# Products over 64 rows, issued once per batch and group of heads instead of once per pair of tiles, in a post-norm transformer block

## The chip, the cores and the metric

The kernel runs on one core of a Trainium2 chip. The core has a matrix engine (TensorE, "PE" in the profile, whose weight loads are a row of their own, "PEld"), three engines for element-wise work (VectorE "DVE", ScalarE "ACT", GpSimd "POOL") and a queue for transfers (SyncE "SP"). Each engine executes its own instructions in the order in which they were emitted, and waits on semaphores for the others. The metric is the device time of one execution in microseconds (us). Three runs of the kernel before gave 1061.97, 1062.08 and 1062.28 us; the median is 1062.08 us.

## The reference

One transformer layer in float32 on an input of 2 batches, 512 tokens and 512 features:

```
q, k, v = x @ Wq.T, x @ Wk.T, x @ Wv.T     # 32 query heads, 8 key/value heads, 128 wide
q, k = rmsnorm(q) * q_norm_w, rmsnorm(k) * k_norm_w
scores = q k / sqrt(128) + slope[head] * (key_pos - query_pos), later keys masked
out = softmax(scores) @ v                  # four query heads share a key/value head
x = layernorm(x + out @ Wo.T)
h = silu(x @ gate.T * gate_s) * (x @ up.T * up_s)       # 1376 wide, integer weights
x = layernorm(x + h @ down.T * down_s)
```

## The kernel before

**Tiling.** The 1024 tokens are 8 tiles of 128 rows, four per batch. A *unit* is (g, b, i): key/value head g (0 to 7), batch b, query tile i (0 to 3) of that batch. Two neighbouring units form a *pair*; there are 64 units and 32 pairs, so a batch and a group g have two pairs: tiles 0 and 1, then tiles 2 and 3. For each pair the main loop (from L1271) emits the projection to q, k and v (`project`), the norms and transposes (`heads`), then for each unit the scores with their softmax (`scores`) and the weighted sum of the values (`attend`), and then the output projection of the pair (`project_out`), which adds into the residual `y`. With the last head, g = 7, the pair's two tiles are normalised (`norm1`). Groups 0 to 5 are visited with the batches inside the group; the last two groups are visited batch by batch. The feed-forward part follows, and its first blocks for batch 0 are placed beside the end of the attention of batch 1.

**Seven products for eight.** Projections (`project`, `project_out`, the feed-forward parts) use Strassen's scheme in Winograd's form (`seven`, L616): seven products of half-sized blocks in place of eight, with sums of operands made on DVE or POOL ahead (for `project_out` the sums `so`, made from `aT` by `sums_a`) and products added up as they leave the accumulators. Product after product goes to one of three accumulator banks a, b, c (`pa_o`, `pb_o`, `pc_o` for the output projection), and each product is added into `y` by DVE (L576) before its bank takes the next one that starts afresh.

**Attention over 64 rows.** A unit's own diagonal block of scores is lower triangular in four strips of 32 queries. For the strips of queries 0 to 63 only the first 64 keys count, for the strips of queries 64 to 127 all 128 keys do. So the product of the diagonal block with the values is split: `attend` multiplies with all 128 rows only for the later queries (L1063), and for the earlier queries of *both* units of a pair the 64 key rows are packed into the two halves of the partitions: `scores` writes the even unit's block into rows 64 to 127 of the odd unit's buffer (`pr_of[i + 1]`, keys `"x"`), they are transposed together into one `prT` tile, and at the end of the odd unit `halves` (L1093) issues two products with 64 rows each, at `tile_position=(k * H2, 0)`: rows 0 to 63 hold the odd unit's block and give its part of the output in bank `px`, rows 64 to 127, against values that were copied to these rows of `vs`, give the even unit's part in bank `pz`; each product is 256 columns wide. `px` is then added into `aT` by DVE, and `pz` is copied (first tile of a batch) or added. The two products of a pair write two different banks: `px` from the ring of transposes `pt` (two banks) and `pz` from the ring `po` (one bank), which also holds `pa`, the accumulator of `attend`.

**What sets the order.** `W.add` records each operation with a planned cost per engine, a priority and the buffers that it reads and writes. `Work.emit` then simulates the engines with these planned costs and emits the operations in the order that results, choosing the engine where an operation may go to more than one (`copy_op`, `tensor`). A buffer is taken from a ring (`ring(stage, name, bufs, shape)`) when its first operation is emitted, and only if a slot is free. So sizes of rings, costs and priorities shape the order on every engine. The program that results is fixed; on the chip, nothing is planned.

**Rings touched.** `kT` and `v` hold keys and values of one (g, b); `prT` (5 slots) the transposed probabilities; `aT` the attention output of a pair; `vs` the shifted values of a pair.

Of the kernel before, what the change touches and what calls it, by code (L numbers as in the profile page):

```python
# [13 lines left out]
ALU = mybir.AluOpType  # L14
# [3 lines left out]
P = 128  # L18
B, S, DM = 2, 512, 512
H, HKV, HD = 32, 8, 128  # L20
G = H // HKV
# [3 lines left out]
NTB = S // P  # L25
# [5 lines left out]
NQ = P // Q  # L31
# [3 lines left out]
H2 = P // 2  # L35
# [12 lines left out]
def pe(n):  # L48
    return max(0.14, n / 600)
# [5 lines left out]
def act(n, scaled=False):  # L55
    return 0.15 + 0.00084 * n + (0.1 if scaled else 0.0)


def dve(n):
    return 0.15 + 0.00106 * n  # L60


def pool_tt(n):
    return 0.27 + 0.00197 * n
# [197 lines left out]
def post_ln_block(  # L262
# [18 lines left out]
    nc = tc.nc  # L281
# [4 lines left out]
    W = Work()  # L286
# [13 lines left out]
    def ring(stage, name, bufs, shape, dtype=F32, gate=None):  # L300
        r = Ring(name, bufs, shape, dtype, gate)
        rings.setdefault(stage, []).append(r)
        return r
# [33 lines left out]

    r_wo = ring("att", "wo", 2, [P, G, DM])
    r_to = ring("att", "to", 1, [P, 4, 2, WO])
    r_kT = ring("att", "kT", 3, [P, S])  # L340
    r_v = ring("att", "v", 3, [P, NTB, HD])
    r_qT = ring("att", "qT", 6, [P, NQ, G, Q])
    r_bias = ring("att", "bias", 2, [P, S])
    r_prT = ring("att", "prT", 5, [P, S])
    r_aT = ring("att", "aT", 2, [P, 2, G, P])
    r_so = ring("att", "so", 1, [P, 4, 2, P])
    r_rel = ring("att", "rel", 1, [P, S])
    r_vs = ring("att", "vs", 2, [P, HD])
    r_pr = [ring("att", f"pr{i}", 1, [P, NQ, (i + 1) * P]) for i in range(NTB)]

    for stage, side in (("all", "left"), ("qkv", "left"), ("att", "right")):
# [12 lines left out]
    A = lambda buf: (buf, 0)  # L364
# [5 lines left out]
    pairs = units[::2]  # L370
# [90 lines left out]
    def load_o(g, prio):  # L461
        wo = Buf(r_wo, f"wo_{g}")
        w_o[g] = wo
        load(
            1.05,
            prio,
            lambda q: q.dma_start(wo.tile, wot[ts(g, G * HD), :].rearrange("(h p) c -> p h c", p=P)),
            [A(wo)],
        )
# [60 lines left out]
    for i in range(NTB):  # L530
# [3 lines left out]
            lambda e, i=i: nc.vector.memset(pr_of[i].tile, 0.0),  # L534
# [36 lines left out]
    def tensor(n, prio, dst, a, b, alu, reads, writes, who=("DVE", "POOL"), sbuf=None, after=()):  # L571
        cost = {"DVE": dve(n), "POOL": pool_tt(n)}
        W.add(
            {e: cost[e] for e in who},
            prio,
            lambda e: vec[e].tensor_tensor(dst(), a(), b(), alu),  # L576
            reads,
            writes,
            after,
            port=len(who) > 1 if sbuf is None else sbuf,  # L580
        )
# [115 lines left out]
    c_of, qTs, kTs, vs, v2s, prTs, aTs = {}, {}, {}, {}, {}, {}, {}  # L697

    def copy_op(n, prio, dst, src, reads, writes, who=("ACT", "DVE")):
        def fn(e):  # L700
            if e == "ACT":
                nc.scalar.copy(dst(), src())  # L702
            else:
                vec[e].tensor_copy(dst(), src())  # L704

        cost = {"ACT": act(n), "DVE": dve(n), "POOL": 0.18 + 0.00086 * n}
        W.add({e: cost[e] for e in who}, prio, fn, reads, writes)
# [316 lines left out]
    def attend(u, prio):  # L1024

        g, b, i = u  # L1030
        key = f"{g}_{b}_{i}"
        pr, v = pr_of[i], vs[g, b]
        p, r = divmod(units.index(u), 2)
        for j in range(i + 1):
            pt, prT = Buf(r_pt, f"pt_{key}_{j}"), Buf(r_prT, f"prT_{key}_{j}")
            prTs[u, j] = prT
            tiles = (2, 3) if j == i and r == 0 else (2, 3, 0, 1) if j == i else (0, 1, 2, 3)
            reads = [(pr, a) for a in tiles]
            if j == i and r:
                reads += [(pr, ("x", a)) for a in range(2)]  # L1040

            def transposes(e, j=j, pt=pt, tiles=tiles):
                for k, a in enumerate(tiles):
                    nc.tensor.transpose(pt[:, ts(k, P)], pr[:, a, ts(j, P)], ident.tile)  # L1044

            n = len(tiles)
            W.add({"PE": n * TR}, prio, transposes, reads + [A(ident)], [A(pt)])
            copy_op(
                n * P,
                prio,  # L1050
                lambda prT=prT, n=n: prT[:, : n * P],
                lambda pt=pt, n=n: pt[:, : n * P],
                [A(pt)],
                [A(prT)],
            )
        po = Buf(r_po, f"pa_{key}")
        for j in range(i + 1):
            prT = prTs[u, j]
            n = S // 2 if j == i else S
            W.add(  # L1060
                {"PE": pe(n)},
                prio + 0.4,
                lambda e, j=j, prT=prT, n=n: nc.tensor.matmul(  # L1063
                    po[:, S - n :],
                    lhsT=v[:, j, :],
                    rhs=prT[:, :n],
                    start=(j == 0),
                    stop=(j == i),
                    skip_group_check=True,
                ),  # L1070
                [A(prT), (v, j)] + ([A(po)] if j else []),
                [A(po)],
            )
        if r == 0:
            aTs[p] = Buf(r_aT, f"aT_{p}")
        aT = aTs[p]
        a0 = 0 if i else 2
        cells = lambda r, lo, hi: aT[:, r].rearrange("p h (a r) -> p a h r", a=NQ)[:, lo:hi]
        rows = lambda t, lo, hi: t.tile.rearrange("p (a h r) -> p a h r", a=NQ, h=G)[:, lo:hi]
        copy_op(  # L1080
            (NQ - a0) * P,
            prio + 0.4,
            lambda: cells(r, a0, NQ),
            lambda: rows(po, a0, NQ),
            [A(po)],
            [(aT, (r, h)) for h in range(a0 // 2, 2)],
        )
        if r == 0:
            return
        prT, v2 = prTs[u, i], v2s[p]  # L1090
        banks = (Buf(r_pt, f"px_{key}"), Buf(r_po, f"pz_{key}"))

        def halves(e):  # L1093
            for k, (bank, val) in enumerate(zip(banks, (v[:, i, :], v2.tile))):
                nc.tensor.matmul(  # L1095
                    bank[:, : S // 2],
                    lhsT=val[k * H2 : (k + 1) * H2],
                    rhs=prT[k * H2 : (k + 1) * H2, S // 2 :],
                    start=True,
                    stop=True,  # L1100
                    tile_position=(k * H2, 0),
                )

        W.add(
            {"PE": 0.64},
            prio + 0.4,
            halves,
            [A(prT), (v, i), A(v2)],
            [A(bank) for bank in banks],
        )  # L1110
        for k, bank in ((1, banks[0]), (0, banks[1])):
            key_k = [(aT, (k, 0))]
            if i - 1 + k == 0:
                copy_op(
                    S // 2,
                    prio + 0.4,
                    lambda k=k: cells(k, 0, 2),
                    lambda bank=bank: rows(bank, 0, 2),
                    [A(bank)],
                    key_k,  # L1120
                )
            else:
                tensor(
                    S // 2,
                    prio + 0.4,
                    lambda k=k: cells(k, 0, 2),
                    lambda k=k: cells(k, 0, 2),
                    lambda bank=bank: rows(bank, 0, 2),
                    ALU.add,
                    [A(bank)] + key_k,  # L1130
                    key_k,
                    ("DVE",),
                )

# [134 lines left out]
    for p in range(NP):  # L1271
        g, b, i = pairs[p]
        u = 2 * p
        if p == first_pair[g]:
            if g > 0:
                load_qkv(g, u - 14.0)
                load_o(g, u - 10.0)
                make_bias(g, u - 2.0)
        if p == 0 or g != pairs[p - 1][0]:
            sums_q(g, u - 3.0)  # L1280
        if p == 0:
            project_plain(p, u - 2.4)
        else:
            if g == 0 or (g == 1 and b == 0 and i == 0):
                sums_x(b, i // 2, u - 3.0, lead if p > 1 else ())
            project(p, u - 2.4)
        heads(p, u - 1.8)
        if p == 0 or g != pairs[p - 1][0]:
            sums_o(g, u + 1.0, lead)
        for k in range(2):  # L1290
            scores(units[u + k], u + k)
            attend(units[u + k], u + k + 0.4)
        project_out(p, u + 2.6)
        if g == HKV - 1:
            for r in range(2):
                norm1(b * NTB + i + r, u + 2.8)

    last_heads = len(W.ops)

# [361 lines left out]
```

## Time and profile before

| What | us |
|---|---|
| Median of three runs | 1062.08 |
| The profiled execution's own time | 1061.77 |
| Its span, first to last instruction | 1060.0 |
| PE busy in the span | 1050.8 |
| DVE, POOL, ACT busy | 654.2, 455.2, 421.6 |
| End of the last PE instruction, from the span's start | 1054.1 |
| Products with 64 rows (L1095): 32 places, four matmul records each | 22.3 (`px` and `pz` at the same time) |

A float32 matmul stands in the trace as two records, two passes over the same data. A record's duration contains the pipeline's fill and drain, so neighbouring records overlap; what a record costs is the distance from its start to the start of the next one, here called its step. The clock that TensorE was granted was 0.999 of full speed over the span.

### The profile page before, as it was taken

The page shows a single profiled execution, that of the slowest core. Times are in us where ns is not written, and L with a number is a line of the kernel's source. Part 1 is how long each engine was busy: PE and PEld are TensorE (multiplying, and loading weights), DVE is VectorE, ACT ScalarE, POOL GpSimd, SP SyncE. Part 2 cuts the span into 40 slices and gives each one's busy share as a digit, 9 for nine tenths or more (in the row PEclk, how much of TensorE's full clock was granted, in tenths as well). Part 3 has the DMA queues.
Part 4 walks back from the last instruction along what each step waited for, and adds up shares of the span by engine and source line. Part 5 has one row for each costly group of instructions (what it writes and reads, how often), then busy time and mean ns, then how long its engine had stood idle before and what let it go on. Part 6 is the DMA issues. An engine that isn't in the chain of part 4 may idle for free.

```text
span 1060.0 us, 13371 instructions
## 1 busy us (share of the span) xinstructions
PE 1050.8 (99%) x4610; PEld 762.2 (72%) x4610; DVE 654.2 (62%) x1603; ACT 421.6 (40%) x1054; POOL 455.2 (43%) x654
## 2 busy tenths in 40 slices
PE   9999999999999999999999999999999999999997
PEld 6676767676767676767676766676767788888886
DVE  6765566556655665566556656666775667667544
ACT  2544444444344434443434343434345333434100
POOL 6854335333533363336324645354664522114220
PEclk9999999999999999999999999999999999999999
DMA  8310012001100110012001100100100022230011
GB/s 258 110 60 1 1 40 60 1 1 41 60 1 1 40 60 1 1 40 61 1 1 40 60 1 1 40 1 1 41 1 22 19 56 85 75 88 21 1 41 40
DMA packets 44307, 38.94 MB, mean 37 GB/s; under 512 B 3696, under 2 KB 36592, under 8 KB 44240
## 3 DMA queue, kind: packets, MB, share of 16 engines
q1 hardware_dynamic: 42512, 37.05, 11.3%
q10 hardware_dynamic: 1728, 1.05, 0.3%
q8 instruction: 36, 0.59, 0.2%
q14 instruction: 31, 0.25, 0.1%
HBM read 35.99 MB, written 2.10 MB: 36 GB/s over the span
## 4 chain that ended last, share of the span: by engine, by line
PE 99%; DVE 0%; issue 0%; ACT 0%; POOLq 0%; POOL 0%
PE pa_q L625 15%; PE sc L955 12%; PE pa L1063 10%; PE pa_o L625 10%; PE pb_q L625 8%; PE pa_h L625 7%; PE pt L1044 6%; PE pb_o L625 5%; PE pc_q L625 4%; PE pb_h L625 4%; PE pa_d L625 3%; PE ptq L902 3%; PE pc_o L625 3%; PE px L1095 2%; PE pc_h L625 2%; PE pb_d L625 2%
## 5 line engine op out<-in xcount | busy, mean ns | idle before, releaser
L1012 POOL TENSOR_SCALAR pr<-pr,rden 128x64 f32<-128x64 f32 (+12 forms) x288 | 138.5, 500 | 56.0 <-DVE rden L995 45.1
L980 ACT ACTIVATE pr<-pr,nmax 128x32 f32<-128x32 f32 (+15 forms) x256 | 132.3, 517 | 63.4 <-DVE nmax L964 60.3
L955 PE MATMUL sc<-kT,qT 128*128 128x160 f32 (+15 forms) x512 | 152.9, 408 | 0.1
L964 DVE CUSTOM_DVE_ANT_0 pr<-sc,bias 128x32 f32<-128x32 f32 (+15 forms) x256 | 110.8, 439 | 64.4 <-PE sc L955 62.8
L1063 PE MATMUL pa<-prT,v 128*128 128x512 f32 (+1 forms) x320 | 136.5, 508 | 0.5 <-ACT prT L702 0.5
L955 PEld LDWEIGHTS sc<-kT,qT 128*128 128x128 f32 x512 | 86.9, 190 | 45.6 <-issue 28.0
L702 ACT COPY prT<-pt 128x512 f32<-128x512 f32 (+1 forms) x112 | 58.6, 529 | 112.7 <-PE pt L1044 111.8
L702 ACT COPY c<-pa_q 128x384 f32<-128x384 f32 x113 | 53.7, 476 | 119.5 <-PE pa_q L625 119.1
L576 DVE TENSOR_TENSOR y<-y,pa_o 128x256 f32<-128x256 f32 x128 | 53.6, 419 | 65.2 <-PE pa_o L625 63.0
L704 POOL COPY v<-c 128x128 f32<-128x128 f32 x51 | 14.9, 292 | 182.7 <-DVE c L576 177.4
L1044 PEld LDWEIGHTS pt<-ident,pr 128*128 128x128 f32 x576 | 69.8, 141 | 30.3 <-issue 20.6
L625 PE MATMUL pa_q<-tq,sx 128*128 128x384 f32 x248 | 90.3, 487 | 0.0
L1044 PE MATMUL pt<-ident,pr 128*128 128x128 f32 x576 | 81.2, 273 | 0.0
L576 DVE TENSOR_TENSOR c<-pb_q,c 128x384 f32<-128x384 f32 x62 | 34.5, 556 | 59.3 <-PE pb_q L625 57.5
L1063 PEld LDWEIGHTS pa<-prT,v 128*128 128x128 f32 x320 | 57.7, 191 | 16.1 <-ACT prT L702 0.7
L625 PE MATMUL pa_o<-to,so 128*128 128x256 f32 x256 | 65.8, 380 | 0.0
L824 ACT ACTIVATE sq<-c 128x640 f32<-128x640 f32 x64 | 47.2, 738 | 45.4 <-DVE c L576 45.3
L625 PEld LDWEIGHTS pa_q<-tq,sx 128*128 128x128 f32 x248 | 45.5, 191 | 27.0 <-issue 7.2
L562 POOL TENSOR_TENSOR inv<-ms,nhalf 128x10 f32<-128x10 f32 (+1 forms) x33 | 63.3, 1917 | 3.8 <-DVE ms L846 2.7
L702 ACT COPY gu<-pa_h 128x256 f32<-128x256 f32 (+1 forms) x88 | 31.8, 370 | 70.7 <-PE pa_h L625 61.9
L625 PEld LDWEIGHTS pa_o<-to,so 128*128 128x128 f32 x256 | 45.3, 191 | 9.5 <-issue 1.0
L704 DVE COPY prT<-pt 128x512 f32<-128x512 f32 (+1 forms) x48 | 32.7, 681 | 27.3 <-PE pt L1044 27.2
(161 smaller groups left out, 2084.9 us busy)
## 6 DMA issues: line engine op xcount, KB each, us to landing
wo<-in_wot_dram SPq DMA_DIRECT2D x8, 1024.0 KB, 5.4
w<-in_wqt_dram SPq DMA_DIRECT2D x31, 256.0 KB, 4.0
wi<-in_gwt_dram SPq DMA_DIRECT2D x14, 256.0 KB, 2.8
wi<-in_uwt_dram SPq DMA_DIRECT2D x14, 256.0 KB, 3.2
wdi<-in_dwt_dram SPq DMA_DIRECT2D x10, 256.0 KB, 3.3
y<-in_x_dram SPq DMA_DIRECT2D x1, 2048.0 KB, 13.0
out_dram<-o SPq DMA_DIRECT2D x8, 256.0 KB, 2.0
w<-in_wkt_dram SPq DMA_DIRECT2D x7, 256.0 KB, 5.0
```

The lines of the kernel that those rows point to most:

```text
L562: lambda e: nc.gpsimd.tensor_tensor(dst(), src(), nhalf[:, :n], ALU.pow),
L576: lambda e: vec[e].tensor_tensor(dst(), a(), b(), alu),
L625: nc.tensor.matmul(bank[:rows, :width], lhsT=a(fa, c), rhs=b(fb, c), start=(fresh and c == 0), stop=(c == depth - 1), skip_group_check=True,)
L702: nc.scalar.copy(dst(), src())
L704: vec[e].tensor_copy(dst(), src())
L824: lambda e, r=r: nc.scalar.activation(sq[:, r].rearrange("p h d -> p (h d)"), c(r)[:, : 5 * HD], AF.Square),
L955: lambda e, a=a, w=w, sc=sc: nc.tensor.matmul(sc[:, :w], lhsT=qT[:, a, :, :], rhs=kT[:, :w], start=True, stop=True),
L964: lambda e, a=a, w=w, sc=sc: nc.vector.tensor_tensor_reduce(out=pr[:, a, :w], in0=sc[:, :w], in1=bg[:, S - w :], scale=-1.0, scalar=MAX_IN ...
L980: lambda e, a=a, w=w: nc.scalar.activation(pr[:, a, :w], pr[:, a, :w], AF.Exp, bias=nmax[:, a : a + 1], scale=-1.0, accum_out=den[:, a : a ...
L1012: lambda e, a=a, c0=c0, n=n, to=to, c1=c1: nc.gpsimd.tensor_scalar(to[:, a, c1 : c1 + n], pr[:, a, c0 : c0 + n], rden[:, a : a + 1], 1.0, ...
L1044: nc.tensor.transpose(pt[:, ts(k, P)], pr[:, a, ts(j, P)], ident.tile)
L1063: lambda e, j=j, prT=prT, n=n: nc.tensor.matmul(po[:, S - n :], lhsT=v[:, j, :], rhs=prT[:, :n], start=(j == 0), stop=(j == i), skip_group ...
```

## The change

The 64-row products of the first pair of a batch and group (tiles 0 and 1) are no longer issued at the end of that pair. They are kept until the end of the second pair (tiles 2 and 3), and then all four products are issued in one operation, one round of two after the other. Each of the two banks is now filled to its 512 columns, the first pair's result in columns 0 to 255 and the second pair's in 256 to 511; the four evictions into the two `aT` buffers follow. `project_out` of both pairs, and `norm1` of all four tiles with the last head, come behind them. The planned cost of the products is 1.07 for four in place of 0.64 for two. The rings of `kT` and `v` shrink from three slots to two, those of `aT` and `vs` grow from two to three.

```diff
-    r_kT = ring("att", "kT", 3, [P, S])
-    r_v = ring("att", "v", 3, [P, NTB, HD])
+    r_kT = ring("att", "kT", 2, [P, S])
+    r_v = ring("att", "v", 2, [P, NTB, HD])
...
-    r_aT = ring("att", "aT", 2, [P, 2, G, P])
+    r_aT = ring("att", "aT", 3, [P, 2, G, P])
...
-    r_vs = ring("att", "vs", 2, [P, HD])
+    r_vs = ring("att", "vs", 3, [P, HD])
...
-        if r == 0:
+        if i < NTB - 1:
             return
-        prT, v2 = prTs[u, i], v2s[p]
+
         banks = (Buf(r_pt, f"px_{key}"), Buf(r_po, f"pz_{key}"))
+        both = [(p - 1, i - 2), (p, i)]
 
         def halves(e):
-            for k, (bank, val) in enumerate(zip(banks, (v[:, i, :], v2.tile))):
-                nc.tensor.matmul(
-                    bank[:, : S // 2],
-                    lhsT=val[k * H2 : (k + 1) * H2],
-                    rhs=prT[k * H2 : (k + 1) * H2, S // 2 :],
-                    start=True,
-                    stop=True,
-                    tile_position=(k * H2, 0),
+            for m, (q, j) in enumerate(both):
+                prT = prTs[(g, b, j), j]
+                for k, (bank, val) in enumerate(zip(banks, (v[:, j, :], v2s[q].tile))):
+                    nc.tensor.matmul(
+                        bank[:, ts(m, S // 2)],
+                        lhsT=val[k * H2 : (k + 1) * H2],
+                        rhs=prT[k * H2 : (k + 1) * H2, S // 2 :],
+                        start=True,
+                        stop=True,
+                        tile_position=(k * H2, 0),
+                        skip_group_check=True,
+                    )
+
+        reads = []
+        for q, j in both:
+            reads += [A(prTs[(g, b, j), j]), (v, j), A(v2s[q])]
+        W.add({"PE": 1.07}, prio + 0.4, halves, reads, [A(bank) for bank in banks])
+        for m, (q, j) in enumerate(both):
+            for k, bank in ((1, banks[0]), (0, banks[1])):
+                dst = lambda q=q, k=k: aTs[q][:, k].rearrange("p h (a r) -> p a h r", a=NQ)[:, :2]
+                src = lambda m=m, bank=bank: bank[:, ts(m, S // 2)].rearrange(
+                    "p (a h r) -> p a h r", a=2, h=G
                 )
-
-        W.add(
-            {"PE": 0.64},
...
+                key_k = [(aTs[q], (k, 0))]
+                if j - 1 + k == 0:
+                    copy_op(S // 2, prio + 0.4, dst, src, [A(bank)], key_k)
+                else:
+                    tensor(
...
-        project_out(p, u + 2.6)
-        if g == HKV - 1:
-            for r in range(2):
-                norm1(b * NTB + i + r, u + 2.8)
+        if i == NTB - 2:
+            for q in (p - 1, p):
+                project_out(q, u + 2.6 - 0.01 * (p - q))
+                if g == HKV - 1:
+                    for r in range(2):
+                        norm1(b * NTB + pairs[q][2] + r, u + 2.8)
```

More of the change, by code (lines that the diff above doesn't have):

```diff
@@ L1104, in attend @@
-        W.add(
-            {"PE": 0.64},
[L1106 to L1133, printed above, removed]
+            for m, (q, j) in enumerate(both):
[10 more added lines that the diff above has]
+                    )
@@ new lines, in attend @@
+        reads = []
[7 more added lines that the diff above has]
+                    "p (a h r) -> p a h r", a=2, h=G
+                )
+                key_k = [(aTs[q], (k, 0))]
[3 more added lines that the diff above has]
+                    tensor(
+                        S // 2,
+                        prio + 0.4,
+                        dst,
+                        dst,
+                        src,
+                        ALU.add,
+                        [A(bank)] + key_k,
+                        key_k,
+                        ("DVE",),
+                    )
```

## The prediction

> **What bounds the kernel now.** I read the page first: engines, granted clock, the chain that ended last.
>
> ```profile
> PE 1050.8 (99%) x4610; PEld 762.2 (72%) x4610; DVE 654.2 (62%) x1603; ACT 421.6 (40%) x1054; POOL 455.2 (43%) x654
> PEclk9999999999999999999999999999999999999999
> PE 99%; DVE 0%; issue 0%; ACT 0%; POOLq 0%; POOL 0%
> ```
>
> PE is busy throughout at full clock and alone makes the chain. Busy records overlap, so I asked next for PE's own waits (total us, times, longest), and for the two long stretches of attention by windows.
>
> ```profile
> PE warm L482 <- POOL ident masks.py:199: 1.3, 1, 1.3
> PE pa_d L625 <- DVE y L576: 0.5, 1, 0.5
> PE pa L1063 <- ACT prT L702: 0.5, 1, 0.5
> PE pa_h L625 <- ACT gu L702: 0.5, 1, 0.5
> PE pa_q L625 <- DVE c L704: 0.4, 1, 0.4
> ```
>
> ```profile
> 60.00:400.00 340.00, 340.00 (x1486) 236.95 (x1485) 203.51 (x522) 146.79 (x375) 148.61 (x222) 1.00 0.09 29
> 400.00:740.00 340.00, 340.00 (x1476) 236.12 (x1475) 208.69 (x525) 147.16 (x373) 151.16 (x222) 1.00 0.06 19
> ```
>
> PE (first column after the length) has no gap between 60 and 740 us; DVE is busy 60%, ACT and POOL 43 to 44%. So only what shortens PE's own sequence counts, and any wait that the change puts on PE counts fully. Then I looked at one place with 64-row products in order of time (start, us, engine).
>
> ```profile
> 90.36 1.46 PE L625 MATMUL pb_q<-tq,sx 128*128 128x384 f32 x4
> 91.74 0.18 PEld L1095 LDWEIGHTS px<-prT,v 64*128 64x128 f32 x1 [0.54 <-issue]
> 91.74 0.48 PE L1095 MATMUL px<-prT,v 64*128 64x256 f32 x1
> 91.75 0.48 PE L1095 MATMUL pz<-prT,vs 64*128 64x256 f32 x1
> 91.84 0.19 PEld L1095 LDWEIGHTS px<-prT,v 64*128 64x128 f32 x1
> 92.06 0.38 PE L1095 MATMUL px<-prT,v 64*128 64x256 f32 x1
> 92.06 0.38 PE L1095 MATMUL pz<-prT,vs 64*128 64x256 f32 x1
> 92.37 0.75 PE L955 MATMUL sc<-kT,qT 128*128 128x288 f32 x2
> 92.96 0.49 PE L625 MATMUL pb_q<-w,sx 128*128 128x384 f32 x1
> ```
>
> For the plain rate, two rows elsewhere with the start of what follows each:
>
> ```profile
> 86.89 1.03 PE L625 MATMUL pa_o<-to,so 128*128 128x256 f32 x4
> 87.75 1.04 PE L1044 MATMUL pt<-ident,pr 128*128 128x128 f32 x8
> ...
> 99.04 1.45 PE L625 MATMUL pa_q<-w,xT 128*128 128x384 f32 x4
> 100.33 0.86 PE L955 MATMUL sc<-kT,qT 128*128 128x416 f32 x2
> ```
>
> Four records of 256 columns take 87.75 - 86.89 = 0.86, so 0.216 each; four of 384 take 1.29, so 0.322 each: 0.84 ns per column.
>
> **What a place with 64-row products costs beyond its columns.** Four steps around it are long. (1) The four `pb_q` records should end at 90.36 + 1.29 = 91.65; `px` starts at 91.74: 0.09, the array runs empty and no weights are loaded ahead. (2) First to second pass of `px`: 0.32 in place of 0.216: 0.10, the weights' loading in the open (the first record lasts 0.48, the second 0.38). (3) `px` to `sc`: 0.31, 0.09 too long: running empty again. (4) Two records of 288 columns should take 2 x 0.243 = 0.49 and take 92.96 - 92.37 = 0.59: 0.10, weights not loaded ahead once more. `px` and `pz` run at the same time, so the pair costs what one of them costs. From the starts in the trace at all 32 places, the means are 0.094, 0.098, 0.090 and 0.104: 0.385 us per place, 12.3 us in all. They do not depend on neighbours: narrow scores after `px` lose the same 0.10.
>
> **The change, part by part.**
>
> *Half of the places go.* Records stay the same in number and columns; 32 places become 16. What must be judged is the second round inside a place. In the row above the second pass of `px` has its weights loaded at 91.84, while the first pass of the same product on the same rows is still running, and its record is the short one: hidden. I take the same for the second round, 0.216 per record: 93 ns before, 320, 216, 216, 313, and 104 behind. Saving: 16 x 0.385 = 6.2 us. A rule speaks against this: the Trainium skill, "TensorE: Matmul & The Clock Gate", Part 3 (What overlaps and what doesn't), says that a weight load overlaps running matmuls only when it is for other rows of the array. By it the second round would show both of its loads, 2 x 0.105, and the saving would be 16 x (0.385 - 0.21) = 2.8 us. The measured row is nearer, since it is the same kind of load in the same mode, so I take 6.2 and keep 2.8 for the range.
>
> *Evictions* stay the same in number (48 additions on DVE at 0.42, 16 copies on ACT at 0.37), but come four at a time and hold `px`'s and `pz`'s banks longer. The cover is PE work placed behind the products. In the new order of instructions, counted with the steps above, the first `project_out` product that reads the copied rows comes 1.03 us or more after the products in the steady stretch. It needs the copy: 0.20 from the stream's end to the eviction's start (a 256-column record lasts 0.16 beyond its step, then 0.04), 0.37, and 0.05 back to PE: 0.62. The next `pa` in `pz`'s bank is 3.4 us away and needs 0.25 + 3 x 0.42 = 1.5, or 2.0 with the 0.56 addition and the 0.85 scaling that stand before them on DVE (these run mostly beside the 1.2 us of products). The sums `so` are first read 3.8 us behind and need 0.4 + 0.42 + 0.73 (POOL) plus handovers, about 1.8. Cost nothing; lost cover would cost each excess 16 times.
>
> *`project_out` twice in succession.* This is the new tight spot. The last products of the first projection (`pa_o`, `pb_o`) are followed at once by the first two of the second in the same two banks, each 0.86 us after its bank's last product, in 15 of 16 places. A bank needs 0.20 + 0.42 (DVE's addition into `y`) + 0.05 = 0.67. Margin 0.19 each. Queued before these additions on DVE are an eviction of a `prT` (0.68, its transposes end as `pa_o` begins: done 0.88 later, before the addition can start at 1.06) for batch 0, and for batch 1 a reciprocal of 0.17 that waits for an exponential done some 0.3 earlier. So no stall. Today's projections have the same 0.86 between products of one bank, and PE shows no wait for them in 680 us.
>
> *Rings.* `kT` and `v` with two slots: the values of a batch are last read by the products at its end, and the next but one batch's first values are copied some 15 us later; nothing waits. The held `prT` leaves four of five slots for the third and fourth units: the order has all transposes 1.3 us or more ahead of their products there, against 0.25 + 0.53 (ACT) or 0.68 (DVE). Transfers and SP's queue keep their order; loads lie several us before use as before.
>
> *The end of attention.* Today PE loses 1.4 us between 806 and 815: 0.33 where `pa` follows `pz` in one bank after 0.43 us, 0.37 on scores behind a busy DVE, and 0.73 on the line "PE pa L1063 <- ACT prT", where a product stands directly behind its transposes. The new order has none of these three, but others at the same place: two transposes 0.44 us after their bank's last use, where evictions need 0.67 and 0.78 (0.3 together, 0.1 for weights), and the 64-row products 0.81 us after the last `pa` in their bank, whose eviction on DVE (0.58) follows three others: 0.4. Sum 0.9, between 0.3 and 2.5. The last normalisation has 4.3 us before PE transposes its rows, against a chain of about 2.9 (two additions and statistics 1.3, small ones 0.4, POOL 0.55, scaling 0.55, handovers); today 6.0 were given and no wait showed. Taken as nothing, at most 1.0. Net: -0.5. The waits at 36, 878 and 1049 us (0.7 to 0.8 each with the weights behind them) stay: the order there is the same, or has another product with no distance to its bank's predecessor (`pa_h`).
>
> **Sum.** Span 1060.0 - 6.2 - 0.5 = 1053.3; the profiled execution has 1.77 outside its span: 1055.1; the median of the runs is 0.31 above that execution: **1055.4 us**, 0.6% faster.
>
> **Rivals.** (a) *The second round's weights are loaded in the open*, as the rule has it: 1062.1 - 2.8 - 0.5 = 1058.8. For it the rule; against it the load at 91.84. (b) *The end of attention is worse*: more new waits from 770 to 855 us, where a bunch of evictions, norms and feed-forward work meets on DVE; with 3.4 us of them in place of the 0.9 that I take, 1055.4 + 2.5 = 1057.9. (c) *Slower: the double projection starves PE.* If one more DVE operation of 0.42 comes before each of the two additions, PE waits 0.42 - 0.19 = 0.23 and then 0.10 for weights, twice in each of 16 places: 10.6 us, 1062.1 - 6.7 + 10.6 = 1066. It decides from 6.7 / 16 = 0.42 us of new wait per place. For it: margins of 0.2, repeated by the schedule; against it: DVE at 60% and the same distance in use today without a wait. (d) *The change doesn't do what it says*: the array empties between the rounds too, and the place costs what two cost: 1061.6.
>
> **How the numbers follow.** Likeliest case 0.74, range of its own 1053.9 to 1057.0 (waits at the end of attention all gone, 1054.5, with 0.6 for what is left unseen, to 1.6 more than taken). (a) 0.10, (b) 0.09, (c) 0.05, (d) 0.02. The range takes in (a) and (b): 1053.9 to 1059.3. About 0.2%, 2.1 us, is what a measurement of this kernel tells from no change. Faster: 0.74 + 0.10 + 0.09 = 0.93; within 0.2%: (d) and some of (c), 0.03; slower 0.04.
>
> **What would show it.** 16 places with eight records (64 `px`, 64 `pz` records as now), inside them steps of 0.32, 0.22, 0.22, 0.31; a step of 0.32 at the third would be (a), 0.4 or more (d). PE still without waits from 60 to 740 us; waits of `pa_o` or `pc_o` on "DVE y" 8 or 16 times would be (c). The wait on `prT` near 814 gone, small ones between 770 and 790 new. The prediction is wrong if PE's waits grow by more than 3 us, or if the steps at a place do not halve in sum.

## The result

The changed kernel takes 1054.88 us (median of six runs, 1054.74 to 1055.31) against 1062.07 us of the kernel before: a ratio of 0.9934, 95% interval 0.9923 to 0.9944. It is faster by 7.2 us, and each of its six runs is below each of the six before. The profiled span went from 1060.0 to 1053.3 us.

The page of the changed kernel: engines, granted clock, and the chain that ended last.

```profile
PE 1044.6 (99%) x4610; PEld 765.6 (73%) x4610; DVE 634.0 (60%) x1598; ACT 422.8 (40%) x1047; POOL 489.3 (46%) x666
PEclk9999999999999999999999999999999999999999
PE 99%; DVE 0%; issue 0%; POOLq 0%; POOL 0%; ACT 0%
```

PE has the same 4610 records, the same mean granted clock (0.999) and is still the whole chain; its busy time is 6.2 us smaller. Its own waits (total us, times, longest), and the two stretches of attention by windows (length, then busy PE, weight loads, DVE, ACT, POOL):

```profile
PE warm L482 <- POOL ident masks.py:199: 1.3, 1, 1.3
PE pa_d L625 <- DVE y L576: 0.5, 1, 0.5
PE pa_h L625 <- ACT gu L702: 0.5, 1, 0.5
PE pa_q L625 <- DVE c L704: 0.4, 1, 0.4
```

```profile
60.00:400.00 340.00, 340.00 (x1508) 241.09 (x1506) 198.38 (x527) 145.76 (x370) 168.43 (x232) 1.00 0.09 29
400.00:740.00 340.00, 340.00 (x1481) 237.69 (x1480) 199.94 (x521) 150.46 (x374) 168.23 (x229) 1.00 0.06 19
```

The wait on `prT` is gone, the two projections in succession cost PE nothing, and in the steady stretch there is no gap. One of the 16 places in order of time (start, us, engine):

```profile
172.17 1.45 PE L625 MATMUL pc_q<-w,xT 128*128 128x384 f32 x4
173.55 0.48 PE L1098 MATMUL px<-prT,v 64*128 64x256 f32 x1
173.56 0.48 PE L1098 MATMUL pz<-prT,vs 64*128 64x256 f32 x1
173.87 0.38 PE L1098 MATMUL px<-prT,v 64*128 64x256 f32 x1
...
174.09 0.38 PE L1098 MATMUL px<-prT,v 64*128 64x256 f32 x1
...
174.30 0.38 PE L1098 MATMUL px<-prT,v 64*128 64x256 f32 x1
...
174.62 0.86 PE L955 MATMUL sc<-kT,qT 128*128 128x160 f32 x4
```

The steps are 0.32, 0.22, 0.21, 0.32: the second round (174.09) costs its columns and nothing else, and its records are all of the short kind, 0.38.

### The profile page after: what moved, and what is told of

Its sections match the earlier page's. It is cut to its first block, busy times and chain, and to the rows that moved or that the text cites. A ratio compares the mean times of both kernels' runs of the same rounds, so it can differ in the third digit from the quotient of the medians.

```text
span 1053.3 us, 13343 instructions
## 1 busy us (share of the span) xinstructions
PE 1044.6 (99%) x4610; PEld 765.6 (73%) x4610; DVE 634.0 (60%) x1598; ACT 422.8 (40%) x1047; POOL 489.3 (46%) x666
## 4 chain that ended last, share of the span: by engine, by line
PE 99%; DVE 0%; issue 0%; POOLq 0%; POOL 0%; ACT 0%
PE pa_q L625 15%; PE sc L955 12%; PE pa L1063 11%; PE pa_o L625 10%; PE pb_q L625 8%; PE pa_h L625 7%; PE pt L1044 6%; PE pb_o L625 5%; PE pc_q L625 4%; PE pb_h L625 4%; PE pa_d L625 3%; PE ptq L902 3%; PE pc_o L625 3%; PE pc_h L625 2%; PE pb_d L625 2%; PE px L1098 2%
## 5 line engine op out<-in xcount | busy, mean ns | idle before, releaser
L955 PE MATMUL sc<-kT,qT 128*128 128x160 f32 (+15 forms) x512 | 148.0, 403 | 0.0
L1012 POOL TENSOR_SCALAR pr<-pr,rden 128x64 f32<-128x64 f32 (+12 forms) x288 | 135.2, 489 | 12.8 <-DVE rden L995 12.4
L702 ACT COPY c<-pa_q 128x384 f32<-128x384 f32 x90 | 42.9, 478 | 140.9 <-PE pa_q L625 139.6
L702 ACT COPY prT<-pt 128x512 f32<-128x512 f32 (+1 forms) x92 | 50.2, 548 | 59.2 <-PE pt L1044 59.0
L704 DVE COPY prT<-pt 128x512 f32<-128x512 f32 (+1 forms) x68 | 42.2, 628 | 42.7 <-PE pt L1044 42.7
L576 POOL TENSOR_TENSOR sq<-c,inv 128x640 f32<-128x640 f32 x54 | 67.2, 1255 | 0.7
L704 POOL COPY v<-c 128x128 f32<-128x128 f32 x36 | 10.5, 291 | 116.7 <-DVE c L576 110.5
L1063 PEld LDWEIGHTS pa<-prT,v 128*128 128x128 f32 x320 | 53.5, 191 | 15.1 <-issue 0.5
L576 POOL TENSOR_TENSOR so<-aT 128x256 f32<-128x256 f32 x32 | 22.9, 726 | 87.8 <-PE pb_o L625 72.3
L909 ACT ACTIVATE qT<-ptq,qw 128x512 f32<-128x512 f32 x61 | 41.9, 687 | 51.6 <-PE ptq L902 50.8
```

Source lines behind the costliest of these rows:

```text
L955: lambda e, a=a, w=w, sc=sc: nc.tensor.matmul(sc[:, :w], lhsT=qT[:, a, :, :], rhs=kT[:, :w], start=True, stop=True),
L1012: lambda e, a=a, c0=c0, n=n, to=to, c1=c1: nc.gpsimd.tensor_scalar(to[:, a, c1 : c1 + n], pr[:, a, c0 : c0 + n], rden[:, a : a + 1], 1.0, ...
L1063: lambda e, j=j, prT=prT, n=n: nc.tensor.matmul(po[:, S - n :], lhsT=v[:, j, :], rhs=prT[:, :n], start=(j == 0), stop=(j == i), skip_group ...
```

## Experiments

The runs fall into three groups; each group ran on one chip together with the kernel before, whose median was 1062.04 to 1062.10 us in the three.

**A visit to the 64-row mode, put back.** The changed kernel with one 128-row transpose between the two rounds.

```diff
             for m, (q, j) in enumerate(both):
+                if m:
+                    nc.tensor.transpose(banks[0][:, S // 2 : S // 2 + P], ident.tile, ident.tile)
...
+        reads += [A(ident)]
```

> The changed kernel with one 128-row transpose of the identity put between the two rounds of 64-row products in each of the 16 places; everything else stands in the same order. It writes columns that the second round overwrites, so the output is the same. Theory (the array's change of mode is what was paid, 0.385 us per visit): each place gains one visit and one transpose, 16 x (0.385 + 0.108) = 7.9 us, 1062.8 us (1061.3 to 1064). Rival (the gain came from the new order of the work): only the transposes count, 16 x 0.108 = 1.7, 1056.6 us.

Its control has the transpose ahead of the place (`if not m`).

> The control for the run before: the same 16 transposes, ahead of the place and not between its rounds. Both theories: 16 x 0.108 = 1.7 us, 1056.6 us. The difference of the two kernels is the price of 16 visits to the 64-row mode without anything else: 6.2 us by the theory, 0 by the rival.

Measured: 1062.2 us with the transpose between, 1056.72 us with it ahead. The same instructions, 5.5 us apart: 0.34 us per visit. The kernel with the transpose between, at one place:

```profile
174.31 0.38 PE L1100 MATMUL px<-prT,v 64*128 64x256 f32 x1
174.31 0.38 PE L1100 MATMUL pz<-prT,vs 64*128 64x256 f32 x1
174.62 0.33 PE L1097 MATMUL px<-ident 128*128 128x128 f32 x1
174.88 0.48 PE L1100 MATMUL px<-prT,v 64*128 64x256 f32 x1
174.89 0.48 PE L1100 MATMUL pz<-prT,vs 64*128 64x256 f32 x1
175.20 0.38 PE L1100 MATMUL px<-prT,v 64*128 64x256 f32 x1
```

All four parts are there again: 0.31 to the transpose (0.097 too long), 0.26 from it to the next `px` (plain is 0.108), and 0.32 to the second pass. The sum in the trace is 0.35 per place, 5.6 us. It is less than 0.385, since the transpose, directly behind 64-row products, shows 0.06 of its weight load and not 0.10 (its load record lasts 0.14 us where others last 0.19). The theory stands; the rival that the order of the work gained falls for this part, since the rest of the order was the same in both.

**The projections alone.** The kernel before, with `project_out` and `norm1` of both pairs behind the second pair and the changed rings, but with the 64-row products at the end of each pair as before.

```diff
-        project_out(p, u + 2.6)
+        if i == NTB - 2:
+            for q in (p - 1, p):
+                project_out(q, u + 2.6 - 0.01 * (p - q))
...
```

> The kernel before with the double output projection alone: project_out and norm1 of both pairs behind the second pair, rings as in the changed kernel, but the 64-row products still at the end of each pair, 32 places. Theory (places are what counts): no gain but the waits at the end of attention, 1062.1 - 0.6 = 1061.5 us (1060.5 to 1063.5). Rival (the order of the projections gained): 1055 to 1057 us. If the double projection starved the matrix engine it would show here too, as over 1064 us.

Measured: 1060.65 us, ratio 0.9987 (0.9980 to 0.9993), within what the theory gave. 32 places, and PE's waits are these:

```profile
PE warm L482 <- POOL ident masks.py:199: 1.3, 1, 1.3
PE pa_q L625 <- DVE c L704: 0.6, 2, 0.4
PE pa_d L625 <- DVE y L576: 0.5, 1, 0.5
```

So two projections in succession do not starve PE either when the places are not joined; and they are worth 1.4 us. By PE's steps in the traces, the 1.4 us of waits at the end of attention and 0.6 at 878 us do not arise in this order; some of that is lost again, 0.4 of it after PE's last product. From here to the changed kernel it is another 5.8 us. The joined places bring 6.5 us of steps, and 1.2 us of waits come back that this order did not have: 0.6 at the end of attention, 0.6 at 878 us. So the 1.4 us are not a part of the changed kernel's gain that could be added to the places.

**The rings alone.** The kernel before with the four changed sizes of rings and nothing else.

> The kernel before with the changed kernel's rings alone (two tiles of keys and of values, three of heads and of shifted values). The order on the matrix engine is that of the kernel before. Theory: the time before, 1062.1 us (1061.5 to 1062.7). Rival (smaller or larger rings count by themselves): more than 1 us away from it.

Measured: 1061.92 us, ratio 0.9999 (0.9991 to 1.0008). By themselves they count for nothing.

**No 64-row products at all.** The kernel before with every diagonal block multiplied with all 128 rows, 0 places in place of 32.

```diff
-            tiles = (2, 3) if j == i and r == 0 else (2, 3, 0, 1) if j == i else (0, 1, 2, 3)
+            tiles = (0, 1, 2, 3)
...
-            n = S // 2 if j == i else S
+            n = S
...
```

> The kernel before without any 64-row product: each diagonal block is transposed and multiplied with all 128 rows, the packing of two units into one tile, the shifted values and the evictions of px and pz are left out; the output is the same. Theory (the sum of steps on the matrix engine): per pair 4 x 0.216 = 0.864 more in pa and 2 x 0.108 more transposes, less 2 x 0.216 + 0.385 for the place, so 0.263 x 32 = 8.4 us: 1070.5 us (1068.5 to 1072). Rival (what the 48 additions and 16 copies took on the other engines counts): nearer to 1062 us.

Measured: 1071.28 us, ratio 1.0086 (1.0071 to 1.0101). The expected sum of PE's steps was 1070.5. The trace has new waits of PE:

```profile
PE pt L1027 <- POOL pr L997: 1.0, 4, 0.3
PE pa L1046 <- DVE prT L704: 0.9, 1, 0.9
```

Three waits that the kernel before has are absent (0.5, 0.5 and 0.4 us), so the listed waits make up 0.5 of the 0.8 us above the sum; the rest was not separated. Half rows are worth 9 us over full rows with a visit per pair, and 16 us with a visit per two pairs.

**The order inside a place.** The changed kernel with its four products issued as `px`, `px`, `pz`, `pz`.

```diff
-            for m, (q, j) in enumerate(both):
-                prT = prTs[(g, b, j), j]
-                for k, (bank, val) in enumerate(zip(banks, (v[:, j, :], v2s[q].tile))):
+            for k, bank in enumerate(banks):
+                for m, (q, j) in enumerate(both):
+                    prT, val = prTs[(g, b, j), j], (v[:, j, :], v2s[q].tile)[k]
```

> The changed kernel with the four products of a place issued as px, px, pz, pz in place of px, pz, px, pz. Theory (instructions start in program order, so only neighbours on different rows run together): the last pass of px runs beside the first of pz, three more steps of 0.216 in each of 16 places, 10.4 us: 1065.3 us, and with no overlap at all 13.8 us, 1068.7 us. If a weight load for the same rows can't be hidden behind a running product, about 0.1 more per such load. Rival (the two row halves run as two queues of their own): no change, 1054.9 us. The steps from px to px show whether the second product's weights are hidden when no product on other rows stands between.

Measured: 1055.07 us, ratio to the kernel before 0.9935 (0.9920 to 0.9950): no change against 1054.88. My expectation failed and the rival held. The trace of one place:

```profile
173.47 0.48 PE L1098 MATMUL px<-prT,v 64*128 64x256 f32 x1
173.49 0.48 PE L1098 MATMUL pz<-prT,vs 64*128 64x256 f32 x1
173.79 0.38 PE L1098 MATMUL px<-prT,v 64*128 64x256 f32 x1
173.81 0.38 PE L1098 MATMUL pz<-prT,vs 64*128 64x256 f32 x1
174.01 0.38 PE L1098 MATMUL px<-prT,v 64*128 64x256 f32 x1
```

`pz` starts 0.014 us behind the first pass of `px`, with three passes of `px` that the kernel emits before it still to come. And the steps of `px` stay at 0.216 with a product on the same rows directly before.

**How far ahead.** To learn whether the two sides are queues of their own, in the kernel just described the first `px` product is issued four times over (the same columns, the same result): ten passes of `px`, then four of `pz`.

> The kernel with px, px, pz, pz in turn, with the first px product issued four times over (each writes the same columns with the same result): five products on rows 0 to 63, then two on rows 64 to 127. If the halves of the rows run as two queues, pz starts beside the first px, and the place lasts as long as its longer side: 5 x 2 x 0.216 = 2.16 in place of 0.864, 16 x 1.30 = 20.7 us more than the changed kernel, 1075.6 us. If pz can start only beside the last px, it lasts 2 x 0.216 x 7 less one overlapped pass, 2.81, 31 us more, 1086 us. The start of pz in the trace, and that there are ten px records and four of pz, tell it without the labels.

Measured: 1077.34 us, between the two, 1.40 us more per place than the changed kernel.

```profile
176.31 1.77 PE L1098 MATMUL px<-prT,v 64*128 64x256 f32 x7
177.71 0.48 PE L1098 MATMUL pz<-prT,vs 64*128 64x256 f32 x1
177.92 0.38 PE L1098 MATMUL px<-prT,v 64*128 64x256 f32 x1
178.03 0.38 PE L1098 MATMUL pz<-prT,vs 64*128 64x256 f32 x1
178.14 0.38 PE L1098 MATMUL px<-prT,v 64*128 64x256 f32 x1
```

In all 16 places `pz` starts 1.405 us after the first `px`, with the seventh of ten passes, so again with three emitted passes overtaken. Both sides finish together but for 0.11 us. So neither theory is right: the sides are not free queues, and starts are not in program order. In both runs a product on other rows overtook three passes, no more and no fewer. Whether the limit is a count of instructions, of loads or of something else was not tried.

**The planned cost of a place.** 1.25 in place of 1.07, so that the planner knows the measured price.

> The changed kernel with the planned cost of a place set to its measured one, 4 x 0.216 + 0.385 = 1.25 in place of 1.07; only the order changes. Theory: in the steady stretch the matrix engine has no waits that a plan could remove, so only the waits at the end of attention and in the feed-forward part can move: 1053.9 to 1055.9 us. Rival (a plan nearer to the measurement is worth more): under 1053.5 us.

Measured: 1054.65 us, ratio to the kernel before 0.9930 (0.9913 to 0.9946), against 1054.88: within the theory's range, and too near the changed kernel to be told from it by these runs.

**A version that beats both.** The remaining small waits of PE stood where a product follows its bank's last use or its transposes at less than 0.7 us, so the planned lag behind PE was raised as well.

```diff
-LAG = {"PE": 0.22, "DVE": 0.1, "ACT": 0.12, "POOL": 0.2, "SP": 0.1, "ACTQ": 0.1, "NONE": 0.0}
+LAG = {"PE": 0.34, "DVE": 0.1, "ACT": 0.12, "POOL": 0.2, "SP": 0.1, "ACTQ": 0.1, "NONE": 0.0}
...
-        W.add({"PE": 1.07}, prio + 0.4, halves, reads, [A(bank) for bank in banks])
+        W.add({"PE": 1.25}, prio + 0.4, halves, reads, [A(bank) for bank in banks])
```

> The changed kernel with two planned numbers set nearer to the trace: a place at 1.25, and the lag from the matrix engine to the next engine 0.34 in place of 0.22; only the order changes. By the order, the products that followed their bank's last use or their transposes after less than 0.7 us are gone but for one in the last projection. Theory: the waits at 36 (0.7), 787 to 796 (0.6) and 877 us (0.7) go, 1054.9 - 2.0 = 1052.9 us (1052.3 to 1054.3). Rival: the longer planned lags cost order elsewhere, 1054.9 us or more.

Measured: 1052.55 us (1052.42 to 1052.81), ratio to the kernel before 0.9910 (0.9893 to 0.9926), below every run of the changed kernel. PE's waits there:

```profile
PE warm L482 <- POOL ident masks.py:199: 1.3, 1, 1.3
PE pa_d L625 <- DVE y L576: 0.5, 1, 0.5
PE pp L721 <- DMA w<-in_wkt_dram: 0.3, 1, 0.3
```

The lines with `pa_q` and `pa_h` are gone, as expected; the one with `pa_d`, which no order of the last projection avoided, stays. By PE's steps in the two traces, with the loads behind the waits, these two account for 1.1 of the 2.3 us, and the end of attention for 0.3. Another 0.4 are the loads behind the places: a transpose follows in 15 of the 16 places, in place of 6. The last 0.5 are the first projection, which came sooner in this profiled execution. The share of each of the two numbers changed was not separated, beyond the run with 1.25 alone.

## Why the prediction was right, point by point

*What bounds the kernel.* Held: PE is the chain before and after, and from run to run the profiled span followed PE's steps to about 0.5 us.

*Half of the places go.* The mechanism held, and the term was a little too small. Predicted were 6.2 us, from four parts of together 0.385 per place. Counted from `px` to `px`, as the row at 91.74 shows it (0.320 and 0.313 between the starts, so 0.104 and 0.097 too long), a place costs 0.398: the means 0.098 and 0.090 left out the 0.007 us by which `pz` starts behind `px`. Summed over all places of the two traces: running empty on entry 3.0 to 1.5 us, the first load 3.3 to 1.7, running empty on exit 3.1 to 1.55, and the load behind 3.35 to 1.4, so 12.7 to 6.1: 6.6 us. The last part fell by more than half, since in 6 of the 16 places a transpose now follows, with its 0.06. The transpose between the rounds and its control gave 0.34 to 0.35 per visit: a visit next to a transpose costs about 0.35, one between other matmuls 0.40.

*The second round is hidden.* I weighed the row with the hidden load against the rule in the Trainium skill ("TensorE: Matmul & The Clock Gate", Part 3) and took the row. It was right: steps of 0.216 in all 16 places. That products on the other rows run in between is not what hides the loads: in the run with five products against two, the first six passes of `px` run with no `pz` beside them, and all steps behind the first are 0.216 (0.32 + 5 x 0.216 = 1.40, from 176.31 to 177.71). By the rule the time would have been 1058.8. The same list says that matmuls start and end in strict program order; the runs with the products in turn show that here the starts do not, for products on different rows: `pz` began 0.014 us behind the first `px` and ahead of three passes.

*Evictions, the double projection, the rings.* Held at nothing: no wait from 60 to 740 us, 1061.92 us with the rings alone, 1060.65 us and no wait of `pa_o` or `pc_o` on `y` with the projections alone.

*The end of attention.* Predicted -0.5, from 1.4 to 0.9. In the trace it went from 1.4 to 0.6: 0.35 at the transposes that find their bank taken (I had 0.4), and 0.25 where the products find their bank taken by the last `pa` (I had 0.4). The place in question:

```profile
798.75 0.48 PE L1098 MATMUL px<-prT,v 64*128 64x256 f32 x1
799.01 0.48 PE L1098 MATMUL pz<-prT,vs 64*128 64x256 f32 x1
```

Only `pz`, whose bank is the late one, starts 0.26 later; `px` runs on. The feared chain of the last normalisation cost nothing.

*The sum.* 1055.4 predicted, 1054.88 measured. By the steps, the places gave 0.5 more than predicted and the end of attention 0.3 more; the runs show 0.5 of these 0.8. The 0.3 between was not traced; what PE loses in the first 20 us differs by up to 0.9 us between the eleven traces. The predicted span, 1053.3, is the measured one to the digit, and that is luck: in this execution the first projection lost 0.8 us more than in the profiled one before, which hid as much of the gain (0.2 came back at 18 us, where the kernel before waited). Some of its first records in the kernel before:

```profile
5.02 0.85 PE L721 MATMUL pp<-w,xT 128*128 128x384 f32 x1
5.66 0.63 PE L721 MATMUL pp<-w,xT 128*128 128x384 f32 x1
6.13 0.49 PE L721 MATMUL pp<-w,xT 128*128 128x384 f32 x1
```

And in the changed one:

```profile
5.03 0.85 PE L721 MATMUL pp<-w,xT 128*128 128x384 f32 x1
5.82 0.98 PE L721 MATMUL pp<-w,xT 128*128 128x384 f32 x1
6.59 0.85 PE L721 MATMUL pp<-w,xT 128*128 128x384 f32 x1
7.23 0.55 PE L721 MATMUL pp<-w,xT 128*128 128x384 f32 x1
```

The early records start 0.64 us and more apart, in place of 0.32, until about 5.8 us in the first and 7.3 us in the second; the two traces record the full granted clock from 5.82 and 7.34 us. The later rise of the clock is 0.55 of the 0.8; for the other 0.28 the profile names no cause. Runs, not one profile, give 7.2.

*The rivals.* (a), (c) and (d) are refuted by the steps and the waits at the places; (b) did not occur. The run without 64-row products shows what a crowded end of attention looks like: 0.9 us for one `prT`.

## What to carry to other kernels

When TensorE is the bound and has no gaps, look at the distances from start to start of its instructions against the columns that they process. Here each visit to the 64-row mode showed there as four surcharges of 0.06 to 0.10 us, and none of them appears among PE's waits. Collect such products until a bank is full, and check that the accumulators and the buffers that wait for it come free in time. Planned costs and lags are worth setting from the trace: two such numbers gave another 2.3 us here.

## What I had not expected of the hardware

The opening says that each engine executes its instructions in the order in which they were emitted. For products on different row halves of the array these runs show otherwise. `pz` began 0.014 us after the first `px`, ahead of three passes of `px` emitted before it, in 15 of 16 places (in the one left over `pz` waited for its bank). With ten passes of `px` in front it began beside the seventh, again ahead of three, in all 16 places. So in these runs neighbours within that distance needed no alternating by hand, but five against two did not overlap fully: 2.46 us from the first product to the instruction behind the place, against 1.07 for two against two.

A weight load left in the open cost 0.10 us before a matmul and 0.06 before a transpose.
